# Two-layer graph network: the closing steps of the second attention, their normalised features on GpSimd instead of ScalarE, and every 28th ramp a comparison instead of every 14th

## The chip, the cores and the metric

The kernel runs on one core of a Trainium2 chip. A core has a matrix engine (TensorE, in the profile PE, with its weight loads as PEld), three elementwise engines (VectorE = DVE, ScalarE = ACT, GpSimd = POOL) and SyncE (SP), which issues most transfers. Each engine takes its instructions strictly in the order in which they were written into its queue; engines wait for each other through semaphores.

The metric is the time of one execution on the device in microseconds (us), as the median over several runs.

## What is computed

A graph of 6250 nodes with 128 features and 200,000 edges, sorted by target node, goes through two layers. Each begins with a normalisation and a maximum with zero; the first is a pair of graph attentions, the second an equivariant convolution:

```python
h = maximum(layernorm(x), 0)
h = elu(gat_layer(h, W1, al1, ar1, b1))        # attention 1: four heads of 16
x = x + gat_layer(h, W2, al2, ar2, b2)         # attention 2: one head, 64 -> 128
h = maximum(layernorm(x), 0)
x = x + convolution(h, edges, edge attributes) # linear parts of h, then messages along edges
```

In `gat_layer` an edge has the weight `exp(leaky_relu(el[src] + er[dst]))`, divided by the sum of the weights over the edges of its target. In the second layer `h` has 32 scalar features and 32 vectors of three, and every node's features pass through the small matrices `W_lin0_*` and `W_lin1_*`, once for the messages and once for the node itself.

## The kernel before, in words

The nodes are cut into 49 blocks of 128 (`NB = 49`, `P = 128`). The program has three large stages. Attention 1 builds, for every pair of blocks, a table `counts` of how many edges run from each node of one block to each node of another, and gathers part of the edges. Attention 2, the stage of the change, makes no gathers: it works densely on the tables. The convolution gathers rows of `table3` by edge, on GpSimd's queue, and takes more than half of the time.

**Attention 2.** The loop over `b0` takes two target blocks at a time. For them it walks over all 49 source blocks in seven groups of `HS = 7`: 25 pairs of targets give 175 groups. Three engines work on a group:

- ScalarE makes a ramp for each source block (line 1398): `relu(STEEP * (er + el))`, with STEEP = 2^60. It is zero where the sum is negative and huge where it is positive.
- VectorE takes the minimum of all ramps of the group with the counts (line 1406, result `up`), so that `up` holds the count where the sum is positive and zero elsewhere; `down` is the count less `up` (line 1407).
- TensorE multiplies `up` and `down` by two sets of weighted features (line 1411, 28 products of 196 columns a group) and adds everything up in PSUM.

`ramp`, `up` and `down` have two buffers each (the pool `dense`). In some groups the ramp of the last source block is left out (`m` is 6 instead of 7); VectorE then makes this block's `up` with a comparison straight from the logits, times the counts (line 1403). Before, that is every group with an odd number, 87 of 175, so every 14th ramp.

**The closing steps.** When two pairs are done, `finish2` closes their four blocks, one step behind each group, as a generator: shares (line 536), transposes (1327), the product with `w2_sb` (1333), the sum with `x` in `xt` (1334), mean and variance (323, 324), `sd` on ScalarE (333), `scale` and `bias` on VectorE (335, 337). Then, for two blocks at a time, the features `h` of the next layer are made: two ScalarE activations a block, one for the 32 scalars (line 1345) and one for the 96 vector parts (line 1346), which also reorders them from (u, i) to (i, u), so it reads every third element. Each is `relu(scale * x + bias)`. TensorE transposes both blocks (344), VectorE copies the result out of PSUM (346), TensorE multiplies by `lin` (1354), ScalarE scales one half into `t3` (1357), VectorE adds the other half to `xt` (1362, 1364), and two transfers write `table3` and `xtd`.

The order on SyncE's queue is written by hand in this stage. On the other engines it is made when the program is built, by a planner that weighs each instruction's expected duration; a changed instruction can therefore change the order of its neighbours.

GpSimd has nothing in this stage but two short memsets at its start (line 1314). The helpers `norm_coefs` and `transposed` are shared with other places; `transposed` takes the copying instruction as an argument (`evict`). `finish2` is also called by `all2`, a fallback that runs only where the tables don't hold (it is in the program, but not run for this input).

Of the kernel before, what the change touches and what calls it, by code (L numbers as in the profile page):

```python
# [36 lines left out]
AF = mybir.ActivationFunctionType  # L37
OP = mybir.AluOpType
# [11 lines left out]
HS = 7  # L50
# [13 lines left out]
def gnn_kernel(ctx: ExitStack, tc: tile.TileContext, x, src, dst, attr4, attr8,  # L64
# [3 lines left out]
    nc = tc.nc  # L68
    N, D = x.shape
    E = src.shape[0]  # L70
    NB = -(-N // P)
# [4 lines left out]
    HID, MUL = Wtp.shape[1], Wtp.shape[2]  # L76
# [97 lines left out]
    xt = pre.tile([P, NB, D], F32, name="xt0")  # L174
# [165 lines left out]
    def transposed(srcs, rows, evict):  # L340

        ps = bank().rearrange("p (j c) -> p j c", j=4)
        for j, s in enumerate(srcs):
            nc.tensor.transpose(ps[:rows, j, :], s, ident)
        t = work.tile([P, 4, P], F32, name="transp")
        evict(t[:rows, :len(srcs), :], ps[:rows, :len(srcs), :])
        return t
# [253 lines left out]
    co = {}  # L601
# [594 lines left out]
    for now in range(NGR * MS + 1):  # L1196
        g, m = divmod(now, MS)
# [61 lines left out]
    xt = ctx.enter_context(tc.tile_pool(name="xt", bufs=1)).tile([P, NB, D], F32, name="xt")  # L1259
# [48 lines left out]
    with tc.tile_pool(name="att2", bufs=1) as pool, tc.tile_pool(name="dense", bufs=2) as dense, \  # L1308
# [10 lines left out]
        def finish2(b0, n):  # L1319
# [11 lines left out]
            ps = bank()  # L1331
# [4 lines left out]
            scale, bias = norm_coefs(fin, b0, n)  # L1336
            t3 = fin.tile([P, 4, D], F32, name="t3")
            for j0 in range(0, n, 2):
                js = range(j0, min(j0 + 2, n))
                m = len(js)  # L1340
                hs = []
                for j in js:
                    h = work.tile([P, D], F32, name="h", bufs=4)
                    co = dict(bias=bias[:, j:j + 1], scale=scale[:, j:j + 1])
                    nc.scalar.activation(h[:, :MUL], xt[:, b0 + j, :MUL], AF.Relu, **co)
                    nc.scalar.activation(h[:, MUL:].rearrange("p (i u) -> p i u", i=3),
                                         xt[:, b0 + j, MUL:].rearrange("p (u i) -> p i u", i=3), AF.Relu, **co)
                    hs.append(h)
                yield
                ht = transposed(hs, D, nc.vector.tensor_copy)  # L1350
                yield
                ps = bank()
                for j in range(m):
                    nc.tensor.matmul(ps[:, j * 2 * D:(j + 1) * 2 * D], ht[:, j, :], lin, start=True, stop=True)
                ps = ps[:, :m * 2 * D].rearrange("p (b j f) -> p b j f", j=2, f=D)
                inv = 1.0 / math.sqrt(MUL)
                nc.scalar.activation(t3[:, j0:j0 + m, :], ps[:, :, 0, :], AF.Copy, scale=inv)
                yield
                cos = math.cos(math.pi / 8.0) * inv
                for j in range(m):  # L1360
                    b = b0 + j0 + j
                    nc.vector.scalar_tensor_tensor(xt[:, b, :MUL], ps[:, j, 1, :MUL], cos, xt[:, b, :MUL],
                                                   op0=OP.mult, op1=OP.add)
                    nc.vector.scalar_tensor_tensor(
                        xt[:, b, MUL:].rearrange("p (u i) -> p i u", i=3),
                        ps[:, j, 1, MUL:].rearrange("p (i u) -> p i u", i=3), cos,
                        xt[:, b, MUL:].rearrange("p (u i) -> p i u", i=3), op0=OP.mult, op1=OP.add)
# [9 lines left out]
        for b0 in range(0, NB, 2):  # L1377
# [14 lines left out]
            for h0 in range(0, NB, HS):  # L1392
                ramp = dense.tile([P, HS, 2 * P], BF16, name="ramp")
                up = dense.tile([P, HS, 2 * P], BF16, name="up")
                down = dense.tile([P, HS, 2 * P], BF16, name="down")
                m = HS - (b0 // 2 * (NB // HS) + h0 // HS) % 2
                for h in range(m):
                    nc.scalar.activation(ramp[:, h, :n * P], erb[:, :n * P], AF.Relu,  # L1398
                                         bias=sel2[:, h0 + h, :], scale=STEEP)
# [170 lines left out]
    with tc.tile_pool(name="conv", bufs=1) as pool, tc.tile_pool(name="gath3", bufs=6) as gath:  # L1570
# [79 lines left out]
        for g, (t, n) in enumerate(groups):  # L1650
            G, g0 = rows
            i = t % LT
# [140 lines left out]
```

## Time and profile before

| | |
|---|---|
| median of 8 runs | 4974.98 us (4954.22 to 5013.07) |
| the profiled execution | 4970.71 us |
| its span, first to last instruction | 4968.9 us |
| busy in the span: TensorE, VectorE, ScalarE, GpSimd | 3216.9, 3514.6, 2851.9, 2474.5 us |
| first ramp of attention 2 starts | 1769.2 us |
| last ramp starts | 2287.1 us |
| first gather of the convolution starts | 2310.2 us |
| busy from 1800 to 2290 us (490 us): TensorE, VectorE, ScalarE | 455.5, 452.1, 477.5 us |
| mean granted TensorE clock, whole span and attention 2 | 0.77 and 1.00 |

How to read the profile's lines. In the groups view, a line is: source line, engine, operation, result <- operands (buffer numbers left out), partitions x elements, number of instances | busy time in us, mean duration of one in ns | idle time of the engine just before them, with what ended it. The duration of one instruction runs from its start to its end; successive instructions of one engine overlap by some tenths of a microsecond, so what one costs its engine is read from one start to the next. In the timeline, the first two columns are the start and the length in us; equal neighbours are merged (x3), and a bracket gives the idle time before and what ended it.

### The profile page before, as it was taken

How to read it: one execution, taken by the hardware profiler on the slowest of the kernel's cores; microseconds unless marked ns; L12 is line 12 of the kernel's file. 1: busy time of each engine (PE TensorE's matmuls, PEld its weight loads, DVE VectorE, ACT ScalarE, POOL GpSimd, SP SyncE). 2: the span in 40 equal slices, each digit the busy share in tenths (PEclk: the TensorE clock that was granted, in tenths of full speed). 3: DMA queues.
4: the chain of work that ended last, by engine and by line, in shares of the span. 5: the costliest groups of instructions: out<-in, count | busy, mean ns of one | idle time of the engine just before them, and what ended most of it. 6: DMA issues, size and time to landing. Idle time of an engine off the chain costs nothing. (4 is left out here: it accounts for less than half of the span.)

```text
span 4968.9 us, 63248 instructions
## 1 busy us (share of the span) xinstructions
PE 3216.9 (65%) x20133; PEld 2277.5 (46%) x20134; DVE 3514.6 (71%) x5878; ACT 2851.9 (57%) x6398; POOL 2474.5 (50%) x2440
## 2 busy tenths in 40 slices
PE   3246676676777689995466656665566656665656
PEld 2245455454555578884234434343333333433334
DVE  5467787687878679994567667676666666676667
ACT  3237787687887679994344444444444444444444
POOL 3655665556665500003556556555555555555652
PEclk7557887788888889997677777776777777777777
DMA  3346666666666554442111111111111111111110
GB/s 98 85 138 168 175 183 171 157 180 167 182 181 177 152 210 161 168 169 72 42 46 50 49 42 50 47 49 45 47 47 47 47 43 46 49 48 47 50 47 22
DMA packets 420330, 491.19 MB, mean 99 GB/s; under 512 B 267914, under 2 KB 303605, under 8 KB 419975
## 3 DMA queue, kind: packets, MB, share of 16 engines
q1 hardware_dynamic: 340900, 345.68, 23.3%
q0 software_dynamic: 78304, 139.36, 12.0%
q8 instruction: 165, 2.70, 0.2%
q10 hardware_dynamic: 770, 1.88, 0.1%
q14 instruction: 191, 1.56, 0.1%
HBM read 383.20 MB, written 103.42 MB: 98 GB/s over the span
## 5 line engine op out<-in xcount | busy, mean ns | idle before, releaser
L351 POOL DMA_INDIRECT G<-table,srcc x1563 | 1474.5, 943 | 1655.1 <-ACT wo_sb L1461 540.0
L351 POOL DMA_INDIRECT G<-table,srcw x808 | 939.1, 1162 | 642.2 <-DVE msg L392 335.6
L1095 ACT ACTIVATE up<-erb,sel 128x512 bf16<-128x512 f32 x1176 | 800.6, 735 | 9.4 <-PE up L1010 9.4
L1476 ACT ACTIVATE hid<-layer 128x512 f32<-128x512 f32 x392 | 232.0, 592 | 881.5 <-remote 609.5
L1522 DVE TENSOR_TENSOR halves<-mess,halves 128x512 fp32r<-128x512 f32 x391 | 267.8, 685 | 549.5 <-ACT halves L1525 432.1
L1473 PE MATMUL layer<-hid,wm_sb 128*128 128x512 f32 x392 | 358.3, 1013 | 377.7 <-ACT hid L1476 254.3
L877 PE MATMUL small<-key,lo 128*128 128x98 bf16 x3136 | 317.2, 234 | 395.7 <-issue 173.4
L859 ACT CAST ca<-small 128x392 bf16<-128x392 f32 x784 | 379.9, 493 | 314.0 <-remote 159.3
L1550 PE MATMUL whole<-halves,ohr 128*128 128x512 f32 x1563 | 554.1, 497 | 0.7 <-ACT acc L1580 0.7
L1010 PE MATMUL up<-up,rc 128*102 128x512 bf16 x1176 | 477.7, 440 | 49.6 <-DMA ctc<-counts 20.0
L877 PEld LDWEIGHTS <-lo 128*128 128x128 bf16 x3136 | 283.3, 124 | 485.7 <-issue 448.6
L1473 PE MATMUL layer<-a8t,wm_sb 16*128 16x512 f32 x392 | 260.5, 749 | 368.1 <-ACT hid L1476 269.0
L1492 ACT ACTIVATE g<-G,a 128x128 f32<-128x128 f32 x1563 | 476.9, 391 | 0.0
L1398 ACT ACTIVATE ramp<-erb,sel 128x256 bf16<-128x256 f32 (+1 forms) x1138 | 458.0, 491 | 13.8 <-DVE up L1406 7.8
L1485 PEld LDWEIGHTS big<-wtp_sb,hid 64*128 64x128 f32 x3126 | 276.0, 260 | 386.8 <-issue 313.6
L1485 PE MATMUL big<-wtp_sb,hid 64*128 64x128 f32 x3126 | 319.8, 363 | 158.4 <-issue 115.4
L1550 PEld LDWEIGHTS whole<-halves,ohr 128*128 128x128 f32 x1563 | 348.6, 231 | 146.7 <-issue 61.7
L1019 DVE TENSOR_TENSOR up<-up,ctc 128x3584 bf16<-128x3584 bf16 x168 | 339.4, 2020 | 100.9 <-ACT up L1095 48.4
L1159 PEld LDWEIGHTS whole<-msg,ohr 128*128 128x128 f32 x1616 | 327.7, 241 | 60.2 <-issue 18.3
L1517 DVE TENSOR_TENSOR mess<-big,g 128x384 f32<-128x384 f32 x391 | 221.4, 566 | 171.8 <-ACT g L1492 143.4
L851 DVE TENSOR_TENSOR lo<-slots,turned 128x2048 bf16<-128x2048 bf16 x196 | 238.4, 1216 | 138.8 <-remote 52.0
L1159 PE MATMUL whole<-msg,ohr 128*128 128x68 f32 x1616 | 322.3, 313 | 2.0 <-ACT ring L1165 2.0
(321 smaller groups left out, 6041.0 us busy)
## 6 DMA issues: line engine op xcount, KB each, us to landing
counts<-ca SPq DMA_DIRECT2D x196, 392.0 KB
ct<-counts SPq DMA_DIRECT2D x196, 392.0 KB
ctc<-counts SPq DMA_DIRECT2D x1344, 56.0 KB
rc<-rhs SPq DMA_DIRECT2D x84, 358.8 KB
oht<-dlow SPq DMA_DIRECT2D x50, 512.0 KB
G<-table,srcc POOLq DMA_INDIRECT x1563
G<-table,srcw POOLq DMA_INDIRECT x808
a8t<-attr_rows SPq DMA_DIRECT2D x391, 16.0 KB
```

The costliest lines, as they stand in the source:

```text
L351: nc.gpsimd.indirect_dma_start(out=G[:, c, :], out_offset=None, in_=table, in_offset=bass.IndirectOffsetOnAxis(ap=idx[:, c:c + 1], axis=0))
L859: nc.scalar.copy(ca[:, :, k * W:(k + WBANK) * W].rearrange("p h (k d) -> p h k d", d=W), ps[:, :WBANK * NKEY].rearrange("p (k h d) -> p h ...
L877: nc.tensor.matmul(ps[:, n * NKEY:(n + 1) * NKEY], lo[:, a, :, r], ky[:, a, :, r], start=True, stop=True)
L1010: nc.tensor.matmul(sums["ups"][j][:2 * C1, :], r[:, i, c:c + 2 * C1], up[:, i], start=h0 + i == 0, stop=h0 + i == NB - 1)
L1019: nc.vector.tensor_tensor(by_part, by_part, state["ct", p, h0].rearrange("p k a h d -> p h (k a) d"), op=OP.min)
L1095: nc.scalar.activation(up[:, i], state["erb", p][:, j], AF.Relu, bias=sel1[:, h0 + i, 2 * q + j:2 * q + j + 1], scale=STEEP)
L1159: nc.tensor.matmul(kept1["acc"], ohs[g][:, t, :], mss[g][:, t], start=g * SB + t == first_of(c), stop=g * SB + t + 1 == last_of(c))
L1398: nc.scalar.activation(ramp[:, h, :n * P], erb[:, :n * P], AF.Relu, bias=sel2[:, h0 + h, :], scale=STEEP)
L1473: keep(nc.tensor.matmul(ph, w, x[:, :npr * P], start=True, stop=True))
L1485: keep(nc.tensor.matmul(pw[:, c, :], hid[half, j * P:(j + 1) * P], wtp_sb[half].rearrange("x p u -> x (p u)"), start=True, stop=True))
L1492: keep(nc.scalar.activation(g0[:, c], G[:, c, :], AF.Copy, scale=a0[:, c, :]))
L1550: keep(nc.tensor.matmul(acc, oh[:, c, :], ms[:, c].rearrange("e s h i u -> e (s h i u)"), start=start, stop=stop))
```

## The change

Three edits, all in attention 2:

- The features `h` of the closing steps are made by GpSimd: two `tensor_scalar` instructions a block (multiply by `scale`, add `bias`) instead of two ScalarE activations. They don't take the maximum with zero.
- The maximum with zero is taken by VectorE in the instruction that copies the transposed features out of PSUM: a `tensor_scalar` with `max` instead of `tensor_copy`.
- The comparison in place of a ramp is made in one group of four (those whose number leaves 1 when divided by 4, 44 of 175) instead of one of two.

```diff
                 for j in js:
                     h = work.tile([P, D], F32, name="h", bufs=4)
-                    co = dict(bias=bias[:, j:j + 1], scale=scale[:, j:j + 1])
-                    nc.scalar.activation(h[:, :MUL], xt[:, b0 + j, :MUL], AF.Relu, **co)
-                    nc.scalar.activation(h[:, MUL:].rearrange("p (i u) -> p i u", i=3),
-                                         xt[:, b0 + j, MUL:].rearrange("p (u i) -> p i u", i=3), AF.Relu, **co)
+                    co = scale[:, j:j + 1], bias[:, j:j + 1]
+                    nc.gpsimd.tensor_scalar(h[:, :MUL], xt[:, b0 + j, :MUL], *co, op0=OP.mult, op1=OP.add)
+                    nc.gpsimd.tensor_scalar(h[:, MUL:].rearrange("p (i u) -> p i u", i=3),
+                                            xt[:, b0 + j, MUL:].rearrange("p (u i) -> p i u", i=3), *co,
+                                            op0=OP.mult, op1=OP.add)
                     hs.append(h)
                 yield
-                ht = transposed(hs, D, nc.vector.tensor_copy)
+                ht = transposed(hs, D, lambda t, ps: nc.vector.tensor_scalar(t, ps, 0.0, None, op0=OP.max))
...
-                m = HS - (b0 // 2 * (NB // HS) + h0 // HS) % 2
+                m = HS - ((b0 // 2 * (NB // HS) + h0 // HS) % 4 == 1)
```

## The prediction

> **What bounds the kernel now.** The change lies wholly in the second attention, so the first thing to find is the limit of that stage. The page's 40 slices show VectorE, ScalarE and TensorE all near full there at a granted clock of 1.00. In the page's costliest groups the ramps carry the first and last start of the stage with them (1769.2 to 2287.1 us in the line's own view), so the stage is some 520 us of the 4968.9 us span:
>
> ```profile
> L1398 ACT ACTIVATE ramp<-erb,sel 128x256 bf16<-128x256 f32 (+1 forms) x1138 | 458.0, 491 | 13.8 <-DVE up L1406 7.8 <-DVEq L497 5.8
> ```
>
> ScalarE hardly ever waits for anything before a ramp (13.8 us in 1138 of them). Second, the stretch view of two rounds. A round is four node blocks, 14 groups of seven ramps, and one set of closing steps (`finish2`); 49 blocks make 12.25 rounds. I cut at two successive starts of the reciprocal of line 335:
>
> ```profile
> 2004.07:2045.55 41.48, 38.98 (x427) 36.75 (x425) 38.63 (x76) 41.05 (x106) 0.00 (x0) 1.00 0.48 169
> 2045.55:2087.03 41.48, 38.98 (x427) 36.74 (x425) 38.63 (x76) 41.04 (x106) 0.00 (x0) 1.00 0.48 169
> ```
>
> The columns are length, then busy time of TensorE, its weight loads, VectorE, ScalarE, GpSimd. The period repeats to the hundredth. ScalarE is busy 41.05 of 41.48 us and sets it; TensorE (38.98) and VectorE (38.63) follow 2.1 and 2.4 us behind. GpSimd does nothing. Third, the timeline of the place that is edited:
>
> ```profile
> 2044.83 0.29 ACT L333 ACTIVATE sd<-mv,eps 128x4 f32<-128x4 f32 x1
> 2046.01 0.15 DVE L337 SCALAR_TENSOR_TENSOR bias<-mv,scale 128x4 f32<-128x4 f32 x1
> 2046.08 0.95 DVE L1406 TENSOR_TENSOR up<-ramp,ct 128x1536 bf16<-128x1536 bf16 x1
> 2046.21 0.41 ACT L1345 ACTIVATE h<-xt,bias,scale 128x32 f32<-128x32 f32 x1
> 2046.52 0.51 ACT L1346 ACTIVATE h<-xt,bias,scale 128x96 f32<-128x96 f32 x1
> 2046.92 0.41 ACT L1345 ACTIVATE h<-xt,bias,scale 128x32 f32<-128x32 f32 x1
> 2047.08 0.14 PEld L344 LDWEIGHTS bank<-ident,h 128*128 128x128 f32 x1 [1.00 <-ACT h L1346]
> 2047.14 1.09 DVE L1407 TENSOR_TENSOR down<-ct,up 128x1792 bf16<-128x1792 bf16 x1
> 2048.16 0.42 DVE L346 COPY transp<-bank 128x256 f32<-128x256 f32 x1
> 2049.86 0.38 ACT L1357 ACTIVATE t<-bank 128x256 f32<-128x256 f32 x1
> 2050.27 0.19 DVE L1362 SCALAR_TENSOR_TENSOR xt<-bank,xt 128x32 f32<-128x32 f32 x1 [1.68 <-ACT t L1357]
> ```
>
> One block's two activations take 0.71 us of ScalarE (start 2046.21 to start 2046.92). TensorE stands 1.00 us at its in-order transpose until the first feature is there. VectorE fills the time from `bias` to the copy (2.0 us) with lines 1406 and 1407, then stands 1.68 us for ScalarE's `t`, which is queued behind eight activations and two ramps.
>
> **The change, part by part.**
>
> *ScalarE.* Off: 49 blocks x 0.71 = 34.9 us. On: the comparison is made in 44 of 175 groups in place of 87, so 43 more ramps; 51 ramps in a row fill 20.49 us in the ScalarE timeline, (20.49 - 0.49) / 50 = 0.40 us each, so 17.2 us. Net -17.7 us, -1.44 us a round: 39.6 us of work where there were 41.05. With the 0.43 us of idle time that it has now, its period would be 40.0.
>
> *VectorE.* Off: 43 comparisons at 0.40 us (2060.34 to the next start at 2060.74) = 17.2 us. On: the minimum of line 1406 over seven heads instead of six in those groups, 1.08 against 0.95 us, 43 x 0.13 = 5.6 us; and the maximum with zero in the copy out of PSUM. For that, line 1291 (a two-operation scalar form out of PSUM, 128x66) takes 264 ns and line 1293 (a plain copy, the same size) 204 ns: 0.06 us x 25 = 1.5 us, from below 0. Sum -10 us, -0.8 a round: 37.8.
>
> *GpSimd.* 98 instructions, eight a round. It ran no such operation, so its price is bounded by its own rows:
>
> ```profile
> L166 POOL IOTA slot_k<- 128x256 bf16 x1 | 1.5, 1535 | 0.0
> masks.py:199 POOL TENSOR_SCALAR_AFFINE_SELECT ident<-ident 128x128 f32<-128x128 f32 x1 | 0.3, 284 | 0.0
> L136 POOL IOTA starts<- 128x50 f32 x1 | 0.2, 177 | 0.0
> ```
>
> Below: the select, the only row that reads and writes a tile, gives 284 ns for 128 columns, so about 0.17 and 0.25 us for 32 and 96. Above: the iota at 6.0 ns a column, 0.2 and 0.6 us. I take 0.2 and 0.3, near the select, which is the like operation: 0.5 us a block, 1.0 for the four instructions that a transposed pair needs, 25 us in all on an idle engine; the upper end is 0.8 a block, 1.6 a pair. Where this is not hidden is what counts, below.
>
> *Two engines at one memory.* What a GpSimd instruction does beside VectorE's bf16 two-input instructions is shown only by the gathers of the first attention:
>
> ```profile
> 1708.48 0.94 POOL L351 DMA_INDIRECT G<-table,srcw  x1 [0.30 <-issue]
> 1712.18 2.01 DVE L1019 TENSOR_TENSOR up<-up,ctc 128x3584 bf16<-128x3584 bf16 x1
> 1712.24 2.77 POOL L351 DMA_INDIRECT G<-table,srcw  x1 [0.30 <-issue]
> ```
>
> 0.94 us alone, 2.77 beside a minimum of the same form as line 1406: 1.83 us more, about what was left of the minimum. The minimum isn't stretched (its 168 instances take 2003 to 2079 ns). So GpSimd can be held for one of lines 1406 and 1407, up to 1.08 us, at each instruction that meets one; where VectorE itself stands waiting for the features, it is held by nothing.
>
> [...]
>
> *Waits in order.* In the built order of the changed kernel nothing changes before or after this stage, nor on the SyncE queue. Inside it the copy (now a maximum) has moved up to `bias`: in seven of 13 rounds nothing stands between them on VectorE, in the others one or two instructions of 0.4 to 1.1 us. The features need 1.0 us of GpSimd, the two transposes 0.41, and three hand-overs of some 0.1: 1.7 us. So VectorE idles 1.7 us in seven rounds and about 0.7 in six, 1.2 on average, where it idled 0; behind it stand the next minima, which free ScalarE's ramp buffers and feed TensorE. From the copy to `t` there are 8 to 14 matmuls (0.084 us each), line 1354 (1.13) and `t` (0.37), about 2.2 us; no minimum stands between in about half of the rounds: 1.2 us on average against 1.68 now. VectorE's idle time is 2.85 a round now (41.48 - 38.63), so 2.85 + 1.2 - 0.5 = 3.6, and its period 37.8 + 3.6 = 41.4.
>
> *TensorE.* Its work stays 38.98. It idles 2.5 us a round now, 1.0 of it for the first feature and 1.0 before line 1327. These waits are in order and stay; if only the small ones go, its period is some 40.5 to 41.
>
> *Sum.* ScalarE 40.0, TensorE 40.5 to 41, VectorE 41.4 if none of its waits is caught up by the two buffers of each ramp tile. I take 40.8: -0.7 us x 12.25 = -8.6 us. The last block, whose chain is bare (2300.81 to the transpose at 2301.68), wins or loses 0.3 us. The profiled execution took 4970.7 us (span 4968.9), 4.3 below the median of the eight runs, so 4962 for it and **4966** against the median of 4974.98.
>
> **Rivals.**
>
> *ScalarE's whole gain comes through.* The waits are absorbed by the double buffers and the stage runs at ScalarE's 39.6 without idle time: -1.9 x 12.25 = -23 us, 4952. For it: VectorE has 1.8 us a round to spare. Against it: TensorE has only 0.6, and its two in-order waits are 2.0.
>
> *The gain is taken by the new waits.* VectorE's 41.4 holds: -0.1 x 12.25 = -1 us, 4974, no change. For it: the empty place behind `bias` in seven rounds.
>
> *GpSimd too slow: slower.* Place: VectorE at the maximum behind `bias`. If each of the four instructions of a pair waits for one of VectorE's 1.08 us minima and then takes 0.25 us, they need 5.3 us, 4.3 more than I allow. VectorE's period is then 41.4 + 4.3 = 45.7 where nothing catches up, and some 44.5 if a quarter does: +3.0 x 12.25 = +37 us, 5012. It decides from where the four need about 2.7 us (0.66 each), at which 41.4 + 1.7 passes 43.1; from 3.0 us on the loss is over 0.5%. For it: the stretched gathers. Against it: in seven rounds VectorE stands still just then, and there is no minimum to wait for.
>
> **How the numbers follow.** A measurement of this kernel tells about 0.5%, 25 us, from no change. My forecast has 0.42, the gain taken by waits 0.18, both within that. ScalarE's whole gain has 0.20; at -23 it lies at the edge, 0.11 beyond and 0.09 within. GpSimd too slow has 0.20, of which 0.18 is over 25 us. So faster 0.11, same 0.71, slower 0.18. Range: down to 4946, the whole gain less the scatter of a median; up to 5006, into the slow rival, leaving out about 0.08 below and 0.12 above; the forecast's own range is 4957 to 4976.
>
> **What would show it.** Right: a round of 40.3 to 41.2 us; ScalarE's busy time near 39.6 and no longer 99% of it; idle time of one to two microseconds on VectorE before the maximum; GpSimd's instructions at 0.2 and 0.3 us; ramps still at 0.40. Wrong: features longer than 0.66 us each on GpSimd, or lines 1406 and 1407 longer than 1.1 us beside them; a round under 40 us, in which the in-order waits cost nothing; or a change outside 1769 to 2310 us, where nothing of the program differs.

## The result and the profile after

The changed kernel takes 5017.26 us (median of 24 runs, 4992.17 to 5066.49) where the kernel before, run beside it, takes 4980.49 (66 runs, 4942.1 to 5042.62). The ratio is 1.0082, its 95% interval 1.0063 to 1.0101: slower by some 40 us, where 4966 had been forecast and the range ended at 5006. The profiled execution took 5018.43 us, its span is 5016.7. (A kernel's executions fall into a faster and a slower state; the ratios in this document compare those of the faster state alone, and none is given where a run has fewer than two.)

The loss lies in the stage that was edited. From the first ramp to the last, attention 2 took 517.9 us (1769.2 to 2287.1); now it takes 556.3 (1780.8 to 2337.1), 38.4 more. The two profiled spans differ by 47.8: the stage also starts 11.6 us later, ahead of any edited instruction, and what follows its last ramp is 2.2 us shorter. First the stretch view of the stage before:

```profile
1769.20:2287.10 517.90, 478.93 (x5154) 448.89 (x5155) 473.48 (x918) 504.34 (x1295) 0.98 (x2) 0.99 0.50 177
```

then that of the changed kernel: the whole stage, and two successive rounds, cut at the reciprocal of line 335 as in the prediction. The columns are length, then busy time of TensorE, its weight loads, VectorE, ScalarE and GpSimd (with the number of instructions), then granted clock, DMA share and GB/s.

```profile
1780.80:2337.10 556.30, 492.71 (x5150) 461.76 (x5151) 467.48 (x874) 493.12 (x1251) 46.19 (x90) 0.96 0.46 165
...
2026.70:2072.10 45.40, 40.09 (x425) 37.73 (x422) 39.39 (x75) 41.54 (x106) 4.07 (x8) 0.96 0.44 155
2072.10:2118.03 45.93, 41.13 (x428) 38.43 (x428) 38.23 (x73) 37.32 (x94) 4.11 (x8) 0.96 0.44 153
```

Every engine has *less* to do than before or the same: ScalarE is busy 493.12 us (504.34 before), VectorE 467.48 (473.48). TensorE's 492.71 (478.93 before) is the same work at a lower clock, 0.96 (0.99 before). Yet these rounds take 45.4 and 45.9 us in place of 41.48, and no engine fills them. So the stage isn't bound by an engine any more; it is bound by waits. Before, ScalarE stood still for 517.9 - 504.3 = 13.6 us of the stage; now for 556.3 - 493.1 = 63.2.

The waits of the changed kernel in this stage (from its waits view, 1781 to 2337 us; the columns after the colon are total us, number of waits, the longest) say for what:

```profile
ACT t L1358 <- PE bank L1355: 33.4, 12, 4.2
...
PE bank L344 <- POOL h L1346: 24.9, 22, 2.5
DVE transp L1351 <- PE bank L344: 23.0, 12, 2.2
DVE up L1407 <- ACT ramp L1399: 21.8, 36, 1.7
...
ACT erb L1118 <- PE small L1116: 11.9, 4, 5.4
...
ACT sd L333 <- DVE mv L324: 9.5, 4, 3.0
```

The same waits before (1769.2 to 2287.1 us), where ScalarE made the features:

```profile
PE bank L344 <- ACT h L1346: 8.5, 10, 1.2
...
ACT sd L333 <- DVE mv L324: 1.5, 1, 1.5
...
DVE transp L346 <- PE bank L344: 1.0, 1, 1.0
...
ACT t L1357 <- PE bank L1354: 0.7, 1, 0.7
```

Three engines now stand still at three successive steps of one chain: TensorE at the transpose until GpSimd has a feature (24.9 us, 8.5 before), VectorE at the maximum until the transpose is done (23.0 us, 1.0 before, at the copy), ScalarE at `t` until the product with `lin` is done (33.4 us, 0.7 before). ScalarE's three lines, `t`, `sd` and `erb`, were 0.7, 1.5 and nothing; they are 54.8 together, 52.6 more, and cover the 49.6 us that its idle time grew by.

One closing of four blocks in the timeline of the changed kernel, the shortest of the eleven in the stage, shows how they stand (start, length, engine and line; in brackets the idle time before, and what ended it):

```profile
2117.70 0.30 ACT L333 ACTIVATE sd<-mv,eps 128x4 f32<-128x4 f32 x1 [2.86 <-DVE mv L324]
...
2118.24 0.16 DVE L337 SCALAR_TENSOR_TENSOR bias<-mv,scale 128x4 f32<-128x4 f32 x1
...
2118.91 0.46 POOL L1346 TENSOR_SCALAR h<-xt,scale,bias 128x96 f32<-128x96 f32 x1
...
2119.42 0.33 PE L344 MATMUL bank<-ident,h 128*128 128x128 f32 x1 [1.82 <-POOL h L1346]
...
2120.57 0.42 DVE L1351 TENSOR_SCALAR transp<-bank 128x256 f32<-128x256 f32 x1 [2.17 <-PE bank L344]
2121.05 1.13 PE L1355 MATMUL bank<-lin,transp 128*128 128x256 f32 x4
...
2122.22 0.38 ACT L1358 ACTIVATE t<-bank 128x256 f32<-128x256 f32 x1 [4.22 <-PE bank L1355]
```

ScalarE makes `sd` at 2117.70, and the next thing in its queue is `t`, which needs the result of the whole chain: reciprocal, bias, four features on GpSimd, two transposes, maximum, product. The chain is bare and takes 2122.22 - 2117.70 = 4.5 us, and ScalarE stands for 4.22 of them with ramps queued behind `t`. Before, five ramps and eight activations stood between the two (three of the ramps ahead of the activations, two behind).

Only two of the eleven closings are as bare as this. In the other nine, 5 to 13 ramps stand between `sd` and `t`, but the chain takes 6.0 to 9.1 us, because its links on VectorE and GpSimd have other work ahead of them or beside them, and `t` still waits 1.4 to 3.9 us. Here with 13 ramps:

```profile
2025.65 0.30 ACT L333 ACTIVATE sd<-mv,eps 128x4 f32<-128x4 f32 x1
...
2025.86 5.28 ACT L1399 ACTIVATE ramp<-erb,sel 128x256 bf16<-128x256 f32 x13
...
2026.73 0.17 DVE L335 RECIPROCAL scale<-sd 128x4 f32<-128x4 f32 x1
...
2027.92 0.15 DVE L337 SCALAR_TENSOR_TENSOR bias<-mv,scale 128x4 f32<-128x4 f32 x1
...
2028.24 1.26 POOL L1345 TENSOR_SCALAR h<-xt,scale,bias 128x32 f32<-128x32 f32 x1 [45.35 <-PE big L1412]
...
2031.28 0.42 DVE L1351 TENSOR_SCALAR transp<-bank 128x256 f32<-128x256 f32 x1 [1.93 <-PE bank L344]
...
2034.80 0.38 ACT L1358 ACTIVATE t<-bank 128x256 f32<-128x256 f32 x1 [3.66 <-PE bank L1355]
```

The minimum stands ahead of the reciprocal and the subtraction ahead of `bias`, 1.1 us each; the first feature takes 1.26 us in place of 0.36, beside VectorE's comparison and minimum. The 13 ramps are over at 2031.14, the chain at 2034.80.

The ramps themselves cost what was forecast; from the groups of the changed kernel's page:

```profile
L1399 ACT ACTIVATE ramp<-erb,sel 128x256 bf16<-128x256 f32 (+1 forms) x1181 | 473.4, 491 | 13.3 <-DVE up L1407 6.6
```

### The profile page after: what moved, and what is told of

Same layout as the page of the kernel before. It is cut to its first block, busy times and chain, and to the rows that moved or that the text cites. A ratio compares the mean times of both kernels' runs of the same rounds, so it can differ in the third digit from the quotient of the medians.

```text
span 5016.7 us, 63304 instructions
## 1 busy us (share of the span) xinstructions
PE 3263.9 (65%) x20133; PEld 2317.0 (46%) x20134; DVE 3510.1 (70%) x5835; ACT 2838.8 (57%) x6343; POOL 2520.8 (50%) x2538
## 5 line engine op out<-in xcount | busy, mean ns | idle before, releaser
L1399 ACT ACTIVATE ramp<-erb,sel 128x256 bf16<-128x256 f32 (+1 forms) x1181 | 473.4, 491 | 13.3 <-DVE up L1407 6.6
```

## The experiments

On the chips of the experiments the kernel before took 4868 to 4883 us, on one of them 4003, and its single times on one chip lay up to 3.3% apart. Much of that lies outside the stage, where no edit reaches: from the last ramp to the end of the span, the profiled executions took 2570 to 2704 us (1998 to 1999 on the chip with 4003). So a whole time can't carry a verdict of 20 us there, and each run is judged by its stage, from the first ramp's start to the last one's in its one trace. The changed kernel is the only one that was traced twice, on two chips: 556.3 and 558.4 us. A difference of some 2 us is taken as none.

| run | what it is | stage, us | ratio of whole times, 95% interval |
|---|---|---|---|
| before, after | | 517.9, 556.3 | after: 1.0082 (1.0063 to 1.0101) |
| e1 | before, every 28th | 530.4 | 1.0183 (1.0088 to 1.0277) |
| e2 | after, every 14th | 556.3 | 1.0082 (1.0018 to 1.0147) |
| e3 | before, 98 spare GpSimd instructions | 520.0 | 1.0103 (0.996 to 1.0245) |
| e4 | after, `t` put late | 550.5 | 1.0133 (1.004 to 1.0225) |
| e5 | e2 in the order of before | 547.4 | 1.0006 (0.9918 to 1.0094) |
| e6 | after in the order of before | 552.8 | 1.0104 (0.9894 to 1.0314) |
| e7 | after, TensorE's stand filled | 551.2 | 0.9952 (0.9872 to 1.0033) |
| e8, e9 | e5, chain shifted by hand | 553.1, 550.4 | one time each, no ratio |
| e10 | e6, shifted as e9 | 562.3 | one time, no ratio |
| e11, e12 | e2, after: new order | 499.5, 515.6 | none; 0.9909 (0.9824 to 0.9995) |
| e13, e14 | before, e1: new order | 523.5, 540.2 | 1.0051 (0.9989 to 1.0113); 0.9948 (0.9876 to 1.002) |
| e15, e16 | e2, after: order mended | 491.6, 503.3 | none; 0.9974 (0.9919 to 1.003) |
| e17 | before: order mended | 514.5 | 1.002 (0.9977 to 1.0062) |
| e18 | after, again | 558.4 | 1.0236 (1.0184 to 1.0287) |

### One part at a time: e1, e2, e3

Is it the ramps, the features on GpSimd, or GpSimd's work beside VectorE's? (In each run the lines of `kernel.py` have numbers of their own.) e1 is the kernel before with the third edit alone, e2 the changed kernel without it:

```diff
-                m = HS - (b0 // 2 * (NB // HS) + h0 // HS) % 2
+                m = HS - ((b0 // 2 * (NB // HS) + h0 // HS) % 4 == 1)
```

e3 is the kernel before with the same 98 GpSimd instructions added, on a tile that nobody reads:

```diff
+                    h0_ = work.tile([P, D], F32, name="h_spare", bufs=4)
+                    co2 = scale[:, j:j + 1], bias[:, j:j + 1]
+                    nc.gpsimd.tensor_scalar(h0_[:, :MUL], xt[:, b0 + j, :MUL], *co2, op0=OP.mult, op1=OP.add)
...
```

> The kernel before with the third part of the change alone: every 28th ramp a comparison in place of every 14th; features by ScalarE, copy by VectorE. Theory (the changed kernel lost because ScalarE's copy t stands behind the whole chain of the features in its order, and ScalarE has no work left to fill it): 43 more ramps of 0.40 us on an engine that was busy for 477.6 of 490 us of this stage, +17 us, about 4997 us, a ratio of 1.003 to 1.004, and no wait of ScalarE at t above 1 us a round. Rival, the ramps are the loss: at least 30 of the 37 us are here, 5010 us or more. Rival, VectorE was the bound: 43 comparisons fewer would make it faster, below 4975 us.

> The changed kernel with the comparison at every 14th ramp kept: features by GpSimd and the maximum in VectorE's copy, ramps as before. Theory: ScalarE loses 2.85 us of work a round, and stands for 3 to 4.5 us a round at t all the same, because t is still 0 to 10 ramps behind sd in its order; 4985 to 5005 us, ratio 1.001 to 1.005, with 35 us or more of ScalarE's waiting at t in this stage. Rival, the engines' sums decide: ScalarE's 35 us come off, or the 20 us down to VectorE's sum, 4945 to 4960 us. Rival, the ramps are the loss: 4980 us or less.

> The kernel before with the change's 98 GpSimd instructions added, each writing a tile of its own that nothing reads; the features still come from ScalarE, and ScalarE's order is that of the kernel before. Theory: GpSimd is held beside VectorE's minima here and there, and nobody waits for it, so no change: 4976 to 4985 us, ratio within 0.001 of 1. Rival, GpSimd takes memory time from VectorE and ScalarE: 98 instructions at up to 0.5 us of delay each, with 10 to 37 us more: 4990 to 5017 us, and minima and subtractions whose mean is longer than the 1.03 and 1.07 us of the changed kernel.

e1: 530.4 us, +12.5. A bound ScalarE pays for most of its 17 us of extra ramps; its idle time fell from 13.6 to 9.8 us. e2: 556.3 us, all of the loss without one extra ramp, so the two parts don't add up: the ramps cost nothing more once ScalarE stands still anyway. (ScalarE waits 39.9 us at `t` in e2, 33.4 in the changed kernel: part of the ramps runs where it had stood.) e3: 520.0 us, +2.1, no more than the two traces of the changed kernel differ by. GpSimd's instructions are held there as well (533 and 630 ns on the mean), VectorE's subtraction stays at 1066 ns on the mean: the rival in which GpSimd takes 10 to 37 us of memory time from the others falls. What costs is not that GpSimd works, but that others wait for it.

### Is it `t` alone? e4

The first form of the theory: `t` comes too soon behind `sd`. In e4 the first pair's chain is put three groups later and tied to the place:

```diff
-                ht = transposed(hs, D, lambda t, ps: nc.vector.tensor_scalar(t, ps, 0.0, None, op0=OP.max))
+                if j0 == 0:
+                    yield from [None] * 3
+                ht = transposed(hs, D, lambda t, ps: tc.keep_in_program_order(nc.vector.tensor_scalar(t, ps, 0.0, None, op0=OP.max)), tc.keep_in_program_order)
...
-                nc.scalar.activation(t3[:, j0:j0 + m, :], ps[:, :, 0, :], AF.Copy, scale=inv)
+                tc.keep_in_program_order(nc.scalar.activation(t3[:, j0:j0 + m, :], ps[:, :, 0, :], AF.Copy, scale=inv))
```

> The changed kernel with all its work, and its chain of closing steps moved: three more steps between the features and the turning of the first pair, and the built order held to the program's order for the transposes, the maximum, the products and t. t then stands 19 to 23 ramps (8 to 9 us) behind sd on ScalarE. Theory: the chain takes 4.5 to 7.8 us from sd to t, so it is over when ScalarE comes to t: its waits at t fall from 47 us to under 10, the half-clock stretches behind TensorE's gaps go with them, and the time is that of ScalarE's sum, 39.6 to 40.8 us a round: 4955 to 4975 us, ratio 0.995 to 0.999. Rival, GpSimd's pace or its sharing of memory: the same instructions run, so the time stays above 5005 us. Rival, the 43 ramps are the loss: 5000 us or more.

550.5 us: missed. `t` now stands 19 to 23 ramps behind `sd` in most closings (36 in two), and its wait does shrink, from 33.4 to 12.6 us. But the waits view of e4 (1716 to 2266 us) has another line ahead of it:

```profile
ACT erb L1118 <- PE small L1116: 29.4, 6, 6.5
...
ACT t L1360 <- PE bank L1357: 12.6, 7, 2.5
...
PE bank L344 <- POOL h L1346: 12.2, 14, 1.3
```

`erb`, the logits of the next pair, waits up to 6.5 us for a TensorE product. At the longest wait (until 1892.88 us) that product stands behind five runs of 14 products that TensorE works off without a gap from 1886.3 to 1892.2: TensorE has fallen behind. So the wait isn't a property of `t`; it moved to another instruction in ScalarE's queue. Why TensorE was behind was not taken apart.

### The order of before: e5, e6

So the theory became: the order, on all three queues. e5 takes e2's instructions and ties TensorE, ScalarE and VectorE to the order of the kernel before (ScalarE's less the 98 features) with edges that only order and wait for nothing; e6 does the same for the whole change.

```diff
+    ORDERS = {
+        'PE': (5046, '196+2 394+2 0+196 606+2 ...
...
+            at = [mine[k] for r in runs.split() for a, n in [map(int, r.split("+"))] for k in range(a, a + n)]
+            for a, b in zip(at, at[1:]):
+                tc.add_manual_dep(b, a.name, mybir.DependencyInfo(mybir.DependencyClass.NoSync,
+                                                                  mybir.DependencyReason.DATA), reason="as before")
```

> Features by GpSimd, maximum in VectorE's copy, every 14th ramp a comparison; and every instruction of TensorE, ScalarE and VectorE in this stage tied to the place in its engine's order that it has in the kernel before (ScalarE's without the 98 feature instructions). Read from the first ramp to the last: 517.9 us in the kernel before, 556.3 in the changed one, 556.3 with the features on GpSimd alone. Theory (the order that was built around the features is the loss, not the engine that makes them): the transposes L344 stand among TensorE's products as before, so its waits there fall from 29 us to 10 or less and the half-clock stretches from 11 to 2 or fewer; ScalarE, without its 2.85 us of features a round, reaches t earlier and stands there for 2 to 3 us a round instead, so nothing is won: 505 to 525 us. Rival, GpSimd's pace or its sharing of memory is the loss: the same GpSimd work with the same results waited for, 545 us or more.

> The whole change (every 28th ramp a comparison too), with TensorE, ScalarE and VectorE in the order of the kernel before; each of the 43 new ramps stands behind the ramp before it. Theory: the new ramps fill part of ScalarE's standing at t or add their 17 us, so 508 to 535 us from the first ramp to the last, with 2 half-clock stretches or fewer. Rival, GpSimd's pace or sharing: 550 us or more. Rival, the ramps are the loss: at least 30 us above the run with every 14th kept.

547.4 and 552.8 us: both missed by far, and inside the ranges that had been set for the rival, GpSimd's pace. ScalarE still waits 63.4 and 55.7 us at `t`. The timeline of e5 shows why the order that was good for ScalarE's features is bad for GpSimd's:

```profile
1995.77 0.30 ACT L333 ACTIVATE sd<-mv,eps 128x4 f32<-128x4 f32 x1
...
1997.03 0.95 DVE L1425 TENSOR_TENSOR up<-ramp,ct 128x1536 bf16<-128x1536 bf16 x1
1997.29 0.93 POOL L1362 TENSOR_SCALAR h<-xt,scale,bias 128x32 f32<-128x32 f32 x1 [39.88 <-PE big L1430]
1998.09 1.09 DVE L1426 TENSOR_TENSOR down<-ct,up 128x1792 bf16<-128x1792 bf16 x1
1998.20 1.31 POOL L1363 TENSOR_SCALAR h<-xt,scale,bias 128x96 f32<-128x96 f32 x1
...
2003.69 0.39 ACT L1375 ACTIVATE t<-bank 128x256 f32<-128x256 f32 x1 [5.62 <-PE bank L1372]
```

The first block's two features last as long as VectorE's minimum and subtraction beside them, the one until 1998.22, the other until 1999.51: 2.2 us where the bare pair takes 0.79. From `sd` to `t` it is 7.9 us, where the kernel before took 2049.86 - 2044.83 = 5.0 for the same steps; and in ScalarE's queue the 2.9 us of features that covered those 5.0 are gone. So the chain became longer and its cover shorter, by about the 5.6 us that ScalarE stands.

### TensorE's clock: e7

In the changed kernel TensorE's stand is followed by stretches at half clock (the last section has the lines), 37.5 us of them there, 34.1 in e2 and 47.8 in e18. e7 keeps each engine's order of the changed kernel and puts six transposes of the constant `ident`, which depend on nothing, ahead of each pair's transposes, into a part of the bank that nobody reads:

```diff
+        dummies = [nc.tensor.transpose(ps[:rows, 3, :], ident, ident).ins for _ in range(fill)]
         for j, s in enumerate(srcs):
```

> The changed kernel in its own order on TensorE, ScalarE and VectorE, with six transposes of the identity that nothing reads (about 1.2 us of TensorE's work) ahead of the features' transposes of each pair of blocks, inside TensorE's standing there. If the half clock that follows such a gap is itself part of the loss: the 11 half-clock stretches of 3.4 us fall to 4 or fewer and each one gone gives back up to 1.7 us, 537 to 548 us from the first ramp to the last, in spite of 30 us more of TensorE's work. If the half clock only happens in time that nobody needs: 553 us or more, however many stretches are left. If TensorE's gaps are not what halves the clock: 9 or more stretches stay.

551.2 us, between the two expectations. Half clock fell from 37.5 to 13.7 us, and the stage by 5.1, with some 30 us of TensorE work put into the stands: net of that work, the clock is a small part of the 38 us. Half clock follows the stand, and most of it goes when the stand is filled.

### Shifting the chain by hand: e8, e9, e10

e8 is e5 with the chain of the first pair later on all three queues (28 products, two bf16 instructions, 12 ramps); e9 also moves the second pair on; e10 is e9 with every 28th. In TensorE's list (first instruction + count; 516 and 517 are a pair's transposes, 546 and 547 its products with `lin`):

```diff
-        'PE': ... 548+40 516+1 588+6 517+1 594+10 546+2 608+19 604+2 627+179 ...
+        'PE': ... 548+56 608+12 516+1 620+6 517+1 626+10 546+2 638+19 604+2 657+9 ...
```

> Features by GpSimd, every 14th ramp a comparison, TensorE, ScalarE and VectorE in the order of the kernel before, as in the run with that order; but in the first 11 groups the features' transposes and products stand 28 of TensorE's products later, the maximum and the update of xt two of VectorE's bf16 instructions later, and ScalarE's t 12 ramps later (17 ramps, 7 us, behind sd). In the run with the unmoved order GpSimd's first block took 2.28 us in place of 0.79 in each round (two of its instructions ran as long as VectorE's minimum or subtraction beside them), TensorE stood 2.3 us at L344, and ScalarE 5.6 us at t. Theory now (a chain that has become longer than the work that covers it, and engines that wait for it in order): with the consumers later, the same chain is covered; L344's waits fall from 24 to under 8 us, t's from 63 to under 12, at most 3 half-clock stretches are left, and the stage takes 500 to 518 us from the first ramp to the last. Rival (GpSimd's pace itself is the loss, wherever its consumers stand): 540 us or more.

> As the run before it in this call, with the second pair of each group moved further than the first (42 products, 3 bf16 instructions) and the updates of xt one more. Theory: no wait is left at the second pair either: 497 to 518 us from the first ramp to the last. Rival, GpSimd's pace: 540 us or more. If the update of xt, which stands behind t, now holds the bank that the next products need: TensorE's wait there grows, 520 to 535 us.

> The whole change, every 28th ramp a comparison, in the order of the second run of this call. Theory: once the stands are gone ScalarE's sum decides again or VectorE's, 43 more ramps take up 1.4 us a round of what the features left free, and VectorE has 2 us less: within 8 us of that run, 497 to 520 us from the first ramp to the last. Rival, the ramps are a loss of their own: 12 us or more above it, as the 43 ramps alone were (530.4 to 517.9).

553.1, 550.4 and 562.3 us: all missed. In e8 the wait at `t` fell to 17.5 us, but VectorE then stood 39.1 us at `xt` for `t`, TensorE 29.6 at the product for the maximum, and the ramps 49.0 for their buffers. The two pairs share one PSUM bank, so every step of the first has to be over before the second begins; three queues can't be set right by moving one step at a time. The first two lie in the range of the rival, GpSimd's pace, and the third, 11.9 us above the second, at the edge of that of the ramps. That was the theory's weak point at that time: no run had yet been *faster* than before.

### A whole order that fits: e11 to e18

Then all three orders were made anew, for each set of instructions by itself: a list in which each engine takes next whatever can start first, with the durations of this case's profiles. The code is e5's, the lists differ. If order is the cause, the changed instructions must be faster than those of before in such an order; if GpSimd's pace or the memory is, no order helps. The kernels of before got an order of the same making, so that the order's own gain isn't put down to the change.

> Features by GpSimd and the maximum in VectorE's copy, every 14th ramp a comparison; TensorE, ScalarE and VectorE in a new order for this stage, in which each engine takes next what is ready first, worked out by adding up the durations of this case's traces (ramp 0.41 us, minimum and subtraction 1.08, feature instructions 0.36 and 0.46 and as long as VectorE's bf16 instruction beside them). No instruction is added or left out against the run with the features on GpSimd alone (556.3 us from the first ramp to the last). Theory (the loss is the place of the chain's links in three in-order queues, not GpSimd's pace): the engine sums, ScalarE 38.6 us a round, VectorE 37.8 and more, TensorE 39, are nearly reached: 475 to 500 us, L344's waits under 8 us, t's under 10, at most 4 half-clock stretches. Rival (GpSimd's pace, its sharing of memory with VectorE, or one PSUM bank through which both pairs pass, keep the stage long in any order): 530 us or more.

> The whole change in an order worked out in the same way. ScalarE has 1.4 us a round more than in the run before it in this call, so its sum, 40.0 us a round, decides: 490 to 515 us from the first ramp to the last, 10 to 20 above that run; the changed kernel took 556.3. Rival, GpSimd's pace or memory or the one bank: 535 us or more.

> The kernel before, instruction for instruction, in an order worked out in the same way: what the order alone is worth without the change. ScalarE's sum of 41 us a round stays: 503 to 518 us from the first ramp to the last (517.9 in the kernel before), 15 to 35 us above the first run of this call if the features on GpSimd are worth what they take off ScalarE. If GpSimd's pace is the loss, this run is the fastest of the four.

> Every 28th ramp a comparison and features on ScalarE, in an order worked out in the same way: 43 more ramps at 0.41 us on the engine with the largest sum, 17 us: 518 to 535 us from the first ramp to the last, and 12 to 20 above the run with every 14th kept. If ScalarE's sum does not decide once the order is right, within 8 us of it.

499.5 us for e2's instructions, 515.6 for the whole change (just over its range): 57 and 41 less than as built. All four have one mistake in common, a product that waits for a transfer, put ahead of the next logits: a single stand of 11.9 to 13.3 us at `erb`, which also took e13 and e14 over their ranges (523.5 and 540.2 us; the 16.7 between them, the price of the ramps, is as expected, and so are the 16.1 between e11 and e12). The next three mend it:

> As the run with the new order, features on GpSimd and every 14th ramp a comparison (499.5 us from the first ramp to the last), with one mistake of that order mended: it put a small product of the convolution's loading ahead of a copy erb, before the transfer it needs had landed, and ScalarE stood 12.9 us there once. With the transfer's 11.5 us counted: 483 to 490 us from the first ramp to the last, and with 517.9 before, 28 to 35 us less for the whole kernel, a ratio of 0.992 to 0.995.

> The whole change in an order mended in the same way (515.6 us from the first ramp to the last with the mistake in it): 499 to 506 us, ratio to the kernel before 0.995 to 0.999, against 1.008 of the change as it was built. If the order is not the cause of that loss, 1.004 or more.

> The kernel before in an order mended in the same way (523.5 us with the mistake in it): 508 to 518 us, ratio 0.998 to 1.001: there is little in the order of the kernel before that could be won, so what the run with GpSimd's features wins is the features' work, not the order.

491.6, 503.3 and 514.5 us. The last two fall into their ranges, the first lies just above its own. The stretch view of the three, each over its own stage (columns as in the first section); first e15:

```profile
1711.70:2203.30 491.60, 470.71 (x5149) 449.12 (x5150) 470.46 (x916) 474.78 (x1207) 75.70 (x90) 0.99 0.52 187
```

then e16, the whole change:

```profile
1719.30:2222.60 503.30, 478.73 (x5151) 445.70 (x5152) 464.60 (x877) 491.07 (x1250) 86.17 (x90) 0.99 0.51 182
```

and e17, the kernel before:

```profile
1714.50:2229.00 514.50, 483.66 (x5153) 447.94 (x5153) 471.18 (x916) 504.96 (x1296) 0.98 (x2) 0.98 0.50 178
```

e16 does the same work as the changed kernel (ScalarE 491.07 us against 493.12, VectorE 464.60 against 467.48) in 503.3 us in place of 556.3. ScalarE is busy 98% of it, as before the change. The instructions are those of the changed kernel, so the 53 us between the two come from the order, with all that follows from it (the waits, the clock). And GpSimd is *slower* in it: its groups in e16 (1719 to 2222 us) have a mean of 1216 and 750 ns,

```profile
L1367 POOL TENSOR_SCALAR h<-xt,scale,bias 128x32 f32<-128x32 f32 x44 | 53.5, 1216 | 394.4 <-DVE bias L337 223.8 <-PE big L1435 140.0 <-issue 30.6
L1368 POOL TENSOR_SCALAR h<-xt,scale,bias 128x96 f32<-128x96 f32 x44 | 33.0, 750 | 0.0
```

where those of the changed kernel (1400 to 2330 us) have 545 and 518:

```profile
L1345 POOL TENSOR_SCALAR h<-xt,scale,bias 128x32 f32<-128x32 f32 x44 | 24.0, 545 | 482.0 <-DVE bias L337 269.3 <-PE big L1412 212.7
L1346 POOL TENSOR_SCALAR h<-xt,scale,bias 128x96 f32<-128x96 f32 x44 | 22.8, 518 | 0.0
```

That costs ScalarE next to nothing, and the timeline of one closing in e16 shows why:

```profile
1989.39 0.30 ACT L333 ACTIVATE sd<-mv,eps 128x4 f32<-128x4 f32 x1
1989.59 8.87 ACT L1422 ACTIVATE ramp<-erb,sel 128x256 bf16<-128x256 f32 x22
1991.52 1.14 POOL L1367 TENSOR_SCALAR h<-xt,scale,bias 128x32 f32<-128x32 f32 x1 [32.13 <-DVE bias L337]
...
1994.31 1.30 POOL L1368 TENSOR_SCALAR h<-xt,scale,bias 128x96 f32<-128x96 f32 x1
...
1997.09 0.41 DVE L1373 TENSOR_SCALAR transp<-bank 128x256 f32<-128x256 f32 x1
...
1998.75 0.38 ACT L1380 ACTIVATE t<-bank 128x256 f32<-128x256 f32 x1 [0.28 <-PE bank L1377]
```

The chain from `sd` to `t` takes 9.4 us here, twice as long as the bare one of the changed kernel. But 22 ramps, 8.87 us, stand between the two in ScalarE's queue, so `t` is 0.28 us late and not 4.22; VectorE too has its minima to do before the maximum, and has no wait there.

> The changed kernel once more, beside these three on one chip: 550 to 560 us from the first ramp to the last, ratio 1.006 to 1.010.

558.4 us, on the chip of e15 to e17, so the 556.3 was no chance; its whole time went further up than expected (1.0236), by more than the stage can explain; what the rest is stays open.

Within orders of the same making, the parts are worth: the features on GpSimd 491.6 - 514.5 = -22.9 us, the ramps 503.3 - 491.6 = +11.7, the whole change -11.2. e15, the first two edits alone, has the shortest stage, 26 us less than the kernel before as built. That the whole kernel gains by it isn't shown: its six runs have a median of 4895 us beside 4883 and scatter from 4734 to 4925.

## Why the prediction was wrong

**The step that failed** is ScalarE's: "With the 0.43 us of idle time that it has now, its period would be 40.0." The work in it was near: -17.7 us had been worked out for 49 blocks, -14.0 for the 44 that close before the last ramp, and the busy time up to there fell by 11.2 in the built orders, by 13.9 in those that fit (491.07 against 504.96). The idle time was not. It went to 63.2 us, 5.2 a round in place of the 1.1 of the whole stage and the 0.43 of the two rounds shown. I had taken the idle time of a bound engine for a constant of the stage. It is the result of an order in which ScalarE's own features, 2.9 us a closing, covered part of the chain that its `t` waits for. Taking them off shortened the cover; held features and other work ahead of the links made the chain longer (6.0 to 9.1 us in nine closings of eleven), and in two closings nothing was left between `sd` and `t`.

**Waits in order** were worked out for VectorE and TensorE, the two engines that the moved work passes through, and not for ScalarE, which it leaves. Even there they were too small: 1.2 us a round before the maximum were allowed, 23.0 us in the eleven closings of the stage were measured, 2.1 each (VectorE's other wait, for `t`, was taken at 1.2 and came to 0.8); "These waits are in order and stay" was said of TensorE, and its wait for the features went from 8.5 to 24.9 us. The numbers needed for it were in the trace of before: `t` had 0.7 us of waits in all, with five ramps and eight activations between it and `sd` in most closings, and the order of the changed kernel shows that the activations go while `t` comes 0 to 13 ramps behind `sd`.

**The sum** took 40.8 us a round; it was 556.3 / 12.25 = 45.4 (517.9 / 12.25 = 42.3 before, by the same count). In the orders that fit, the change is worth -11.2 us (e17 to e16), near the -8.6 of the sum; but there ScalarE, busy 98%, sets the time, where the sum had TensorE's and VectorE's waits do it, so that agreement is partly luck.

**GpSimd's price** was too low: 0.2 and 0.3 us were taken, 0.36 and 0.46 were measured where VectorE's two-input instructions were not beside them, and the narrow form lies above its own bound of 0.2. Together a block takes 0.79 us from start to start in place of 0.5, just inside the upper end of 0.8. It doesn't decide.

**Two engines at one memory** was right for GpSimd: it is held for what is left of VectorE's two-input instruction (0.36 and 0.46 us become 0.93 to 1.39 in e5, and up to 2.2 in the changed kernel and in e16). That VectorE's instruction isn't stretched, which the gathers showed, doesn't hold here. Where GpSimd comes first, VectorE is held too, in the changed kernel for instance by 0.23 us (such a subtraction takes 1.09 alone):

```profile
2031.85 0.46 POOL L1346 TENSOR_SCALAR h<-xt,scale,bias 128x96 f32<-128x96 f32 x1
2031.93 1.32 DVE L1408 TENSOR_TENSOR down<-ct,up 128x1792 bf16<-128x1792 bf16 x1 [0.23 <-PE big L1412]
```

Where the GpSimd instruction isn't held itself, the excess in this trace is what is left of it less some 0.14 us: 0.38 us left and 0.23 more here, 0.20 and 0.06 at 1935.98, 0.19 and 0.04 at 2076.56. But few instructions meet like this, and the excess adds up to 0.5 us in the stage of the changed kernel; line 1408 takes 1073 ns on the mean, 1069 before. What the step of the wide form costs was not shown: 96 columns at a step of 12 bytes take 0.455 us at the shortest and 32 columns at a step of 4 take 0.358, and two durations don't tell a price of the step from the fixed part of an instruction. If the step costs nothing they fit, as an estimate, 0.31 us and 1.5 ns a column.

**VectorE's maximum** was to cost 0.06 us a copy; it costs none: 421 ns on the mean in the stage against 423 for the copy.

**The rivals.** ScalarE's whole gain (4952) and the gain taken by waits (4974) both took too little from the waits. "GpSimd too slow" forecast 5012, 5 us from what came, but by another mechanism: its place was VectorE at the maximum, and it was to decide from 0.66 us for each instruction. In the changed kernel they take 0.55 and 0.52 us on the mean, below that, and the time is lost; in e16 they take 1.22 and 0.75, above it, and the stage is 53 us shorter. Its time was nearly right by coincidence.

**What would show it.** The ramps stayed at 0.40 us and lines 1407 and 1408 at 1.04 and 1.07 on the mean (single ones up to 1.32), and outside the stage nothing was lost but the 11.6 us ahead of it in the one profile. The round, 45.4 us, was outside the 40.3 to 41.2, and GpSimd's instructions were longer than the 0.2 and 0.3 us.

What stays open: why the planner puts `t` where it does, and the share of each of the four causes in the built order (the missing cover, the chain made longer by held features and by work ahead of its links, the shared bank, the clock, of which e7 gives the last as some 5 us net of the work put in). That the order as a whole is the cause is shown by e16 beside the changed kernel: the same instructions, 503.3 us against 556.3 and 558.4.

## What to carry to other kernels

Work on a bound engine may also be the cover of a serial chain that this engine waits for later in its own queue. Before moving it to an idle engine, take the chain from the last input to the waiting instruction (here `sd` to `t`, 4.5 to 9 us), and count what is still queued between the two on each in-order engine; what is missing is lost at each closing, however idle the new engine is. Take the chain as long as it is in the new order, with the work queued ahead of its links, and not as long as it is bare. And where a planner makes the order, judge a change to the work in orders made for each version; here the order moved 53 us and the change itself 11.

## What the runs showed of the hardware

**Half clock after a stand.** All 970 changes of TensorE's granted clock in the traces of before and of the changed kernel lie, within 0.01 us, on a grid of 3.41 us. Three successive windows of this grid in the changed kernel (stretch view; the clock is the third number from the end):

```profile
2068.41:2071.82 3.41, 3.41 (x42) 3.28 (x40) 3.40 (x9) 3.38 (x10) 0.00 (x0) 1.00 0.02 5
2071.82:2075.23 3.41, 0.43 (x4) 0.14 (x2) 1.70 (x4) 3.37 (x9) 2.60 (x5) 1.00 0.56 171
2075.23:2078.65 3.42, 3.42 (x16) 3.05 (x17) 1.55 (x2) 0.00 (x0) 1.52 (x4) 0.50 1.02 332
```

TensorE was busy for 0.43 us of the second; in the third it gets half its clock, and 16 matmuls fill it where 42 filled the first. Of the windows of the changed kernel's stage at full clock, 14 have at most 1.7 us of work, and 11 of these were followed by one at half clock, all of those up to 1.49 us; of those with 2.0 us or more, none. The kernel before has one window under 1.8 us there (1.36), and it too is followed by one at half clock. Over the whole of these two traces, 382 of the 386 windows at full clock with less than 1.48 us of work (43%) are followed by half clock, and 52 of the 1,070 with 1.76 us (52%) or more; in between it goes either way (46 of 69). So here a window less than half busy was nearly always enough.

**Held, and free.** 98 GpSimd instructions beside a VectorE that is busy 91% of the stage (473.48 of 517.9 us before) cost nothing that shows where nobody waited for them (e3, +2.1 us), though in the changed kernel each engine was held beside the other (GpSimd up to 2.2 us in place of 0.46, VectorE by up to 0.23 us). The maximum in the instruction that empties PSUM cost nothing (421 ns, 423 for the copy).

**Overlap by idle time.** The same 43 ramps cost 12.5 us where ScalarE is the bound (e1), 11.7 to 16.7 in the orders that fit (e15 to e16, e11 to e12, e13 to e14), and nothing between e2 and the changed kernel, where ScalarE stands still anyway (556.3 both).
